# Fetches of pre_u's rows add to cleared tiles instead of copying into them, in a four-layer graph network

## The chip, the cores and the metric

The kernel runs on one core of a Trainium2 chip. The metric is device time in microseconds, measured over several executions; the median of 9 is 3608.16 us (3602.16 to 3622.97). The engines are TensorE (PE, with its weight loads as PEld), VectorE (DVE), ScalarE (ACT), GpSimd (POOL) and SyncE (SP). All values are float32.

## The reference, cut to what matters

The input x holds 64 graphs of 256 nodes with 256 features; adj is one sparse 256x256 matrix for all of them. Layers 0, 1 and 3 are of one kind, layer 2 is an attention over all nodes.

```python
def gnn(h, adj, W1, b1, W2, b2, Wa, ba, Wm, bm, beta1, beta2, beta3):
    pre_u = h @ W1[:256]
    pre_v = h @ W1[256:]
    hidden = relu(pre_u[:, :, None, :] + pre_v[:, None, :, :] + b1)   # one row per pair of nodes (u, v)
    S = sigmoid((hidden @ W2)[..., 0] + b2[0])
    a = einsum('buv,bud->bvd', S * adj, h)
    m = einsum('uv,bud->bvd', adj, h) * h
    return beta1 * h + beta2 * (a @ Wa + ba) + beta3 * (m @ Wm + bm)

x = gnn(x, layer 0); x = gnn(x, layer 1); x = attention(x); x = gnn(x, layer 3)
```

S is needed only where adj is not zero. For each edge (u, v) the kernel must form one row of 256 values, pre_u[u] + pre_v[v] + b1, take the relu, and multiply with W2.

## The kernel before

Two graphs are worked on at a time as a pair, and two pairs are under way side by side: side a takes pairs 0, 4, 8 and so on, side b pairs 2, 6, 10. `beside` joins the scores of one side ("heavy") with all other steps of the other side ("light") into one instruction order, which every engine keeps. One such round is called a block below. There are 96: 32 pairs times three GNN layers, in the order layer 0 of a, layer 0 of b, layer 1 of a, layer 1 of b, layer 3 of a, layer 3 of b. These six are called A0, B0, A1, B1, A3 and B3. Beside B1 and A3 the light steps hold an attention.

The edges of the matrix are sorted into 16 tiles of up to 128 edges, and a tile holds the edge rows of both graphs (128 partitions by 2 x 256). There are two ways to fill a tile. Eight tiles (`FAST`) are made by TensorE: ScalarE puts rows of pre_u and pre_v into the tile pre (`rows_u`, line 727, and `rows_v`, line 736), and one product with the 0/1 matrix pick gives the sums (line 675). The other eight (`FETCHED`) are gathered by GpSimd from two tables in DRAM. SyncE writes pre_u and pre_v with b1 to these tables (line 613), and `fetch` issues two indirect DMAs per tile (line 719): one copies the u rows into the tile, and one adds the v rows (`compute_op=(ALU.bypass, ALU.add)[x]`). A small ninth tile, left, holds edges that fit nowhere else and is filled in the same two steps.

`FETCHES` fixes the order of these 18 issues per block: four u fetches, four v fetches, then left's u, three u, left's v, one u and the last four v. The first eight use only the first 128 table rows. They are issued in `before`, right after these rows are written, and their tiles are called fetched of their side. The other ten are issued at the start of `scores`, and go to a fetched tile that both sides share. GpSimd works in this order and waits, where it must, for the table (SP's DMA), for the u rows of the same tile, and for the readers of a tile that is used again.

VectorE reads each edge row once (line 639: relu, times W2, summed into raw). `got` walks the eight fetched tiles, `made` the eight products. Then `rated_all` turns the sums into scores on ScalarE (lines 659 and 660), once for the first half of the tiles (EARLY) and once for the second (LATE), and VectorE multiplies them with the edges' weights into rm (line 667). In the next block, where this side is the light one, `spread` (line 763) brings rm back to matrix form with matmuls, VectorE adds it into sa (line 765), and `finish` goes on with sa (line 278), aT (line 338), the products with Wm and Wa (line 360 or 346), the new hT (line 363) and h. `before` of the next layer then computes pre_u and pre_v (line 608), evacuated as pu by ScalarE (line 609) and pv by VectorE (line 610).

Of the kernel before, what the change touches and what calls it, by code (L numbers as in the profile page):

```python
# [14 lines left out]
P = 128  # L15
# [60 lines left out]
def adj_seq_kernel(ctx: ExitStack, tc: tile.TileContext, a: dict, out: bass.AP):  # L76
# [186 lines left out]
    def stages(pools):  # L263
        fm, wk, one, ps, ga = (pools[k] for k in ("fm", "wk", "one", "ps", "ga"))


        feats = [one.tile([P, 2, D + 2], FP, name=f"f{g}") for g in range(2)]
        for f in feats:
            nc.gpsimd.memset(f[:, :, D + 1 : D + 2], 1.0)
# [59 lines left out]
        def finish(st, l):  # L329

            sa, mT = st["sa"], st["mT"]
            few_scores = l == GNN[1]
            hb = kept(st, l)
            aT = one.tile([P, 2, 2, N], FP, tag="aT", name="aT")
            for g in range(2):
                t = psum()
                product(t, st["h"][g], sa[:, :, g, :])
                nc.scalar.copy(aT[:, :, g, :], t)  # L338
                yield 0 if few_scores else 1
            if l == LAST:  # L340
                for g in range(2):
                    z = psum()
                    for m in range(2):
                        for j, (w, y) in enumerate(((wm[l], mT), (wa[l], aT))):
                            for c in range(2):
                                mm(out=z[:, m, :], lhsT=y[:, c, g, blk(m)], rhs=w[:, c, :],  # L346
                                   start=j == 0 and c == 0, stop=j == 1 and c == 1)
                        yield m * (1 + g), 1
                    o = h_tile(st, g)
                    nc.vector.tensor_tensor(o, hb[:, g], z, ALU.add)  # L350
                    nc.sync.dma_start(
                        out=out[bass.ds(st["b"] + g, 1)].rearrange("b (c p) d -> p (b c) d", p=P), in_=o
                    )
                return
            hT = hT_tile(st)
            for m in range(2):
                z = psum()
                for j, (w, y) in enumerate(((wm[l], mT), (wa[l], aT))):
                    for c in range(2):
                        mm(out=z, lhsT=w[:, c, blk(m)], rhs=y[:, c], start=j == 0 and c == 0, stop=j == 1 and c == 1)  # L360
                    if j == 0:
                        yield 0
                nc.vector.tensor_tensor(hT[:, m], hb[:, m], z, ALU.add)  # L363
                yield m if few_scores else (2 * m, 1)
            st["hT"] = hT
            st["h"] = []
            for g in range(2):
                t = psum()
                flip(t, hT[:, :, g, :])
                h = h_tile(st, g)  # L370
                if l == GNN[1]:

                    nc.vector.tensor_tensor(h, t, bias2.unsqueeze(1).to_broadcast([P, 2, D]), ALU.add)
                else:
                    nc.scalar.copy(h, t)
                st["h"].append(h)
                yield 0 if few_scores else (g, 1)
# [62 lines left out]
                    yield 0, 1  # L440
                st["h"].append(h)

        return dict(psum=psum, product=product, load=load, mixed=mixed, finish=finish, attention=attention)

    def few(stack):
        pools = open_pools(stack)
        wk, one, ga = pools["wk"], pools["one"], pools["ga"]
        s = stages(pools)  # L450
        psum, mixed, finish, attention, load = (s[k] for k in ("psum", "mixed", "finish", "attention", "load"))

# [9 lines left out]
        ids_v = one.tile([P, len(FETCHED)], I32, name="ids_v")  # L464
        left_u = one.tile([P, 1], I32, name="left_u")
        left_v = one.tile([P, 1], I32, name="left_v")
        tables = stack.enter_context(tc.tile_pool(name="tables", bufs=1, space=bass.MemoryType.DRAM))
        diag = one.tile([P, 2, N], FP, name="diag")
        nc.gpsimd.affine_select(
# [4 lines left out]
        def edges():  # L474
            scratch = Scratch(*(
                (one.tile([P, n * 2 * D], FP, tag=tag + "b", name="scratch"), n * 2 * D)
                for tag, n in (("pre", len(FAST)), ("fetched", FIRST))
            ))
            flat = lambda: psum().rearrange("p a b -> p (a b)")
            first, last, begin, number = numbers  # L480
            place = scratch.tile([P, P], FP, name="place")
# [103 lines left out]
        def before(st, l):  # L585

            hT = st["hT"]
            pu = one.tile([P, 2, 2, D], FP, tag="pu" + st["side"], name="pu")
            pv = one.tile([P, 2, 2, D], FP, tag="pv" + st["side"], name="pv")
            pre = one.tile([P, len(FAST), 2 * D], FP, tag="pre" + st["side"], name="pre")  # L590
            flat = lambda t: t.rearrange("p m g d -> p m (g d)")
            order = [(m, g) for m in range(2) for g in range(2)]
            if l == LAST:
                order = [(m, g) for g in range(2) for m in range(2)]
            st["tables"] = [
                tables.tile([N, 2 * D], FP, tag="table" + t + st["side"], name="table" + t) for t in "uv"
            ]

            own = one.tile([P, 2, 2, D], FP, tag="own", name="own")
            st["pu"], st["pv"], st["pre"], st["own"] = pu, pv, pre, own  # L600
            t = one.tile([P, FIRST, 2, D], FP, tag="fetched" + st["side"], name="fetched")
            st["fetched"] = [t[:, f] for f in range(FIRST)]
            for m, g in order:
                if l == LAST and (m, g) == (1, 0):
                    st["flip"](1)
                t = psum()
                for c in range(2):
                    mm(out=t, lhsT=hT[:, c, g, blk(m)], rhs=w1[l][:, c], start=c == 0, stop=c == 1)  # L608
                nc.scalar.copy(pu[:, m, g, :], t[:, 0, :])  # L609
                nc.vector.tensor_tensor(pv[:, m, g, :], t[:, 1, :], b1row[l], ALU.add)  # L610
                if g == 1:
                    for rows, x in zip(st["tables"], (pu, pv)):
                        nc.sync.dma_start(out=rows[blk(m)], in_=flat(x)[:, m])
                    if m == 0:
                        st["fetches"] = list(FETCHES)

                        if numbered:
                            fetch(st, 2 * FIRST)
                nc.vector.tensor_tensor(own[:, m, g, :], t[:, 0, :], pv[:, m, g, :], ALU.add)
                if g == 1:  # L620
                    if m == 0:
                        rows_u(st, 0, 2, 0, 0)
                    rows_v(st, 2 - 2 * m, 2, 0)
                yield 0, (m, g) != order[1]
            yield REST_OF_IT
            yield from mixed(st, l)

        def scores(st, l):
# [17 lines left out]

            own = st["own"]
            st["left"] = left = one.tile([P, D], FP, tag="left", name="left")
            t = one.tile([P, len(FETCHED) - FIRST, 2, D], FP, tag="fetched", name="fetched")
            st["fetched"] += [t[:, f] for f in range(len(FETCHED) - FIRST)]  # L650
            fetched = st["fetched"]
            fetch(st, len(FETCHES))

            def tile_scores(t, k, m, i):
                col = BLOCKS + 16 * m + 4 * k + i
                both(t, col, col + 8)
# [30 lines left out]
            def got(made):  # L687
                for f, block in enumerate(FETCHED):
                    if f == FIRST:
                        for _ in made:  # L690
                            yield
                        rated(left, REST)
                        rated_all(EARLY, 0)
                        yield
                    tile_scores(fetched[f], *block)
                    if f == FIRST + 1:
                        early(st)
                    yield

            def end():  # L700
                rated_all(LATE, 1)
                past.append(st["rated"].ins)

            made = made()
            return made, got(made), end

        def fetch(st, n):

            now, st["fetches"] = st["fetches"][:n], st["fetches"][n:]
            for f, x in now:  # L710
                rows = st["tables"][x]
                if f < 0:
                    to, ids = st["left"], (left_u, left_v)[x]
                    rows = rows.rearrange("n (g d) -> (n g) d", g=2)
                else:
                    to, ids = st["fetched"][f].rearrange("p g d -> p (g d)"), (ids_u, ids_v)[x][:, f : f + 1]
                    if f < FIRST:
                        rows = rows[blk(0)]
                nc.gpsimd.indirect_dma_start(  # L719
                    out=to, out_offset=None, in_=rows, in_offset=bass.IndirectOffsetOnAxis(ap=ids, axis=0),  # L720
                    compute_op=(ALU.bypass, ALU.add)[x],
                )

        def rows_u(st, f, n, k, m):
# [87 lines left out]
        for _ in steps(a_[0]):  # L812
            pass
        edges()
        numbered.append(True)
        other_weights(one, psum)
        while a_[1] is not None:
# [105 lines left out]
```

## Time and profile before

| | |
|---|---|
| median of 9 executions | 3608.16 us (3602.16 to 3622.97) |
| profiled execution | 3604.12 us, its span 3602.3 us |
| TensorE clock granted, mean | 0.989 |
| busy: PE, DVE, ACT, POOL | 3472.6, 2604.4, 1599.5, 2228.8 us |
| HBM traffic | 162 GB/s over the span |

The page of a profile gives the busy time of each engine, the DMA queues, and groups of equal instructions: line, engine, operation, output and inputs, number, busy time, mean of one in ns, and after the second bar the time in which the engine was idle just before them, with what ended it. Other views show the same trace as a timeline, or as busy times per stretch. A record on POOL is the time in which GpSimd issues one indirect DMA; the rows land later, which only the DMA's own packet records or a waiting engine show.

### The profile page before, as it was taken

To read this page: it belongs to the slowest core of one execution; us is meant where nothing else is said; L and a number is where in the kernel's file an instruction comes from. 1 tells how busy PE (TensorE), PEld (TensorE's weight loads), DVE (VectorE), ACT (ScalarE), POOL (GpSimd) and SP (SyncE) were. 2 spreads that over 40 slices of the span, in tenths; PEclk is the share of its full clock that TensorE was granted. 3 is DMA by queue.
4 is the path that set the end of the run, shared out by engine and by line. 5 is a ranking of instruction groups with operands and counts; after the bars stand their busy time and mean duration, and the time that the engine had idled before them with its cause. 6 is when DMAs were issued, how large, how long until landed. Compare 5 with 4: busy or idle time off the path is not lost. (4 is left out here: it accounts for less than half of the span.)

```text
span 3602.3 us, 48531 instructions
## 1 busy us (share of the span) xinstructions
PE 3472.6 (96%) x14328; PEld 2116.3 (59%) x14328; DVE 2604.4 (72%) x10584; ACT 1599.5 (44%) x2929; POOL 2228.8 (62%) x1754
## 2 busy tenths in 40 slices
PE   7999999999999999999999999999999999999998
PEld 4555565655656556565565656556565665655555
DVE  5667676776767777777776767768677777777676
ACT  2444444444444444444444444444444444444352
POOL 3746657576665756566576665765757566665754
PEclk8999999999999999999999999999999999999999
DMA  5757677686777767677687776867767676776865
GB/s 153 166 140 178 156 166 166 150 181 153 179 155 172 167 144 187 150 177 177 146 184 157 171 171 151 180 156 178 160 156 176 149 183 151 175 174 143 182 149 114
DMA packets 303918, 587.27 MB, mean 163 GB/s; under 512 B 37536, under 2 KB 103968, under 8 KB 303648
## 3 DMA queue, kind: packets, MB, share of 16 engines
q0 software_dynamic: 190464, 427.93, 58.8%
q1 hardware_dynamic: 111600, 154.96, 12.4%
q8 instruction: 117, 1.92, 0.2%
q14 instruction: 153, 1.25, 0.1%
q10 hardware_dynamic: 1584, 1.20, 0.1%
HBM read 466.51 MB, written 117.44 MB: 162 GB/s over the span
## 5 line engine op out<-in xcount | busy, mean ns | idle before, releaser
L719 POOL DMA_INDIRECT fetched<-tableu,ids_u x768 | 767.2, 999 | 987.5 <-DMA tableu<-pu 773.3
L719 POOL DMA_INDIRECT fetched<-tablev,ids_v x768 | 1207.3, 1572 | 257.5 <-issue 235.6
L675 PE MATMUL ga<-pre,pick 128*128 128x512 f32 x1536 | 768.1, 602 | 5.8 <-DVE junk L639 3.2
L639 DVE SCALAR_TENSOR_TENSOR junk<-ga,L_gnn_w2row 128x256 f32<-128x256 f32 x1536 | 584.9, 420 | 158.1 <-PE ga L675 127.3
L608 PE MATMUL ps<-L_gnn_w,hT 128*128 128x512 f32 x1536 | 689.3, 598 | 8.7 <-DMA hT<-in_xT_dram 8.7
L639 DVE SCALAR_TENSOR_TENSOR junk<-fetched,L_gnn_w2row 128x256 f32<-128x256 f32 x1536 | 606.9, 419 | 41.1 <-DMA fetched<-tablev,ids_v 39.7
L736 ACT COPY pre<-pv 64x512 f32<-64x512 f32 x768 | 473.4, 616 | 106.6 <-DVE pv L610 73.9
L608 PEld LDWEIGHTS ps<-L_gnn_w,hT 128*128 128x128 f32 x1536 | 288.8, 192 | 355.9 <-issue 331.4
L278 PE MATMUL ps<-sa,h 128*128 128x256 f32 x1536 | 393.6, 398 | 66.3 <-DVE sa L765 50.7
L278 PEld LDWEIGHTS ps<-sa,h 128*128 128x128 f32 x1536 | 290.7, 196 | 219.2 <-DVE sa L765 110.3
L727 ACT COPY pre<-pu 64x1024 f32<-64x1024 f32 x384 | 392.9, 1038 | 3.8
L363 DVE TENSOR_TENSOR hT<-hb,ps 128x512 f32<-128x512 f32 x128 | 88.1, 688 | 414.3 <-PE ps L360 312.1
L675 PEld LDWEIGHTS ga<-pre,pick 128*128 128x128 f32 x1536 | 277.9, 191 | 166.4 <-issue 130.5
L278 PE MATMUL ps<-adj,h 128*128 128x256 f32 x1536 | 359.0, 386 | 4.0 <-PE ps L278 1.8
L278 PEld LDWEIGHTS ps<-adj,h 128*128 128x128 f32 x1536 | 283.2, 190 | 73.7 <-issue 27.5
L609 ACT COPY pu<-ps 128x256 f32<-128x256 f32 x384 | 141.7, 372 | 413.4 <-PE ps L608 356.4
L324 ACT ACTIVATE hb<-hT,L_gnn_zbias,scas 128x512 f32<-128x512 f32 x128 | 97.4, 807 | 498.8 <-DVE hT L363 348.8
L338 ACT COPY aT<-ps 128x512 f32<-128x512 f32 x192 | 112.4, 586 | 442.5 <-PE ps L278 395.7
L667 DVE TENSOR_TENSOR rm<-gva,val 128x256 f32<-128x256 f32 x768 | 284.1, 419 | 1.7
L360 PE MATMUL ps<-aT,L_gnn_Wa 128*128 128x512 f32 x512 | 240.6, 592 | 0.0
L360 PE MATMUL ps<-mT,L_gnn_Wm 128*128 128x512 f32 x512 | 240.6, 592 | 0.0
L763 PEld LDWEIGHTS ps<-rm,gu 128*64 128x64 f32 x3072 | 175.4, 138 | 107.2 <-issue 52.4
(155 smaller groups left out, 4186.4 us busy)
## 6 DMA issues: line engine op xcount, KB each, us to landing
tableu<-pu SPq DMA_DIRECT2D x192, 256.0 KB
tablev<-pv SPq DMA_DIRECT2D x192, 256.0 KB
h<-in_x_dram SPq DMA_DIRECT2D x64, 256.0 KB
hT<-in_xT_dram SPq DMA_DIRECT2D x64, 256.0 KB
out_dram<-h SPq DMA_DIRECT2D x64, 256.0 KB
fetched<-tableu,ids_u POOLq DMA_INDIRECT x768
fetched<-tablev,ids_v POOLq DMA_INDIRECT x768
L_gnn_w<-in_L_gnn_W_dram SPq DMA_DIRECT2D x6, 256.0 KB
```

What stands on the lines that cost most here:

```text
L278: mm(out=o[:, m, :], lhsT=lhs[:, c, blk(m)], rhs=rhs[:, c, :], start=c == 0, stop=c == 1)
L338: nc.scalar.copy(aT[:, :, g, :], t)
L360: mm(out=z, lhsT=w[:, c, blk(m)], rhs=y[:, c], start=j == 0 and c == 0, stop=j == 1 and c == 1)
L608: mm(out=t, lhsT=hT[:, c, g, blk(m)], rhs=w1[l][:, c], start=c == 0, stop=c == 1)
L609: nc.scalar.copy(pu[:, m, g, :], t[:, 0, :])
L639: nc.vector.scalar_tensor_tensor(junk, t, 0.0, w2row[l], ALU.max, ALU.mult, accum_out=raw[:, i : i + 1])
L667: nc.vector.tensor_tensor(rm[:, k, ms, g, :], gva[:, k, ms, :], val[:, i : i + 4].unsqueeze(2).to_broadcast([P, 4, 64]), ALU.mult)
L675: mm(out=t, lhsT=pick[:, k, 4 * m + i, :], rhs=pre[:, n], start=True, stop=True)
L719: nc.gpsimd.indirect_dma_start(out=to, out_offset=None, in_=rows, in_offset=bass.IndirectOffsetOnAxis(ap=ids, axis=0), compute_op=(ALU.byp ...
L727: nc.scalar.copy(st["pre"][h, f : f + n], st["pu"][h, m].rearrange("p g d -> p (g d)").unsqueeze(1).to_broadcast([64, n, 2 * D]),)
L736: nc.scalar.copy(st["pre"][halves[1 - k], n], st["pv"][halves[i % 2], i // 2].rearrange("p g d -> p (g d)"))
L763: mm(out=t[h, :, quarter(i)], lhsT=gu[:, k, 4 * m + i, :], rhs=rm[:, k, 4 * m + i], start=True, stop=True)
```

## The change

The u fetches add as well, so a tile must be zero before its first fetch. The fetched tiles are three fixed tiles now, ahead for each side (tiles 0 to 3) and behind for both (tiles 4 to 7). ScalarE clears them in halves by copying a column of zeros, broadcast: ahead in `before`, placed behind the last copy of aT (`done`), and behind in `end`, placed after the late scores. The left tile is filled as before: its u rows are copied. The scratch memory of `edges` uses the side b tile of ahead in place of its predecessor.

```diff
@@ stages
+        done = []
...
-                nc.scalar.copy(aT[:, :, g, :], t)
+                done.append(nc.scalar.copy(aT[:, :, g, :], t).ins)
@@ few
+        zero = one.tile([P, 1], FP, name="zero")
+        nc.gpsimd.memset(zero, 0.0)
+        ahead = {side: one.tile([P, FIRST, 2 * D], FP, name="ahead" + side) for side in "ab"}
+        behind = one.tile([P, len(FETCHED) - FIRST, 2 * D], FP, name="behind")
+
+        def place_of(st, f):
+            return (ahead[st["side"]], f) if f < FIRST else (behind, f - FIRST)
+
+        def fetched(st, f):
+            t, f = place_of(st, f)
+            return t[:, f].rearrange("p (g d) -> p g d", g=2)
+
+        def clear(t, start, end):
+            nc.scalar.copy(t[:, start:end], zero.unsqueeze(2).to_broadcast([P, end - start, 2 * D]))
@@ before
-            t = one.tile([P, FIRST, 2, D], FP, tag="fetched" + st["side"], name="fetched")
-            st["fetched"] = [t[:, f] for f in range(FIRST)]
+            for f in range(0, FIRST, 2):
+                with tc.issue_after(done[-1]) if done else nullcontext():
+                    clear(ahead[st["side"]], f, f + 2)
@@ scores
-            t = one.tile([P, len(FETCHED) - FIRST, 2, D], FP, tag="fetched", name="fetched")
-            st["fetched"] += [t[:, f] for f in range(len(FETCHED) - FIRST)]
-            fetched = st["fetched"]
             fetch(st, len(FETCHES))
...
-                    tile_scores(fetched[f], *block)
+                    tile_scores(fetched(st, f), *block)
...
             def end():
                 rated_all(LATE, 1)
                 past.append(st["rated"].ins)
+                with tc.issue_after(past[-1]):
+                    for f in (0, 2):
+                        clear(behind, f, f + 2)
@@ fetch
-                    to, ids = st["fetched"][f].rearrange("p g d -> p (g d)"), (ids_u, ids_v)[x][:, f : f + 1]
+                    to, ids = fetched(st, f).rearrange("p g d -> p (g d)"), (ids_u, ids_v)[x][:, f : f + 1]
...
-                    compute_op=(ALU.bypass, ALU.add)[x],
+                    compute_op=ALU.bypass if (f, x) == (-1, 0) else ALU.add,
@@ after edges()
+        for f in (0, 2):
+            clear(behind, f, f + 2)
```

More of the change, by code (lines that the diff above doesn't have):

```diff
@@ L441, in attention @@
                 st["h"].append(h)
-        return dict(psum=psum, product=product, load=load, mixed=mixed, finish=finish, attention=attention)
+        return dict(psum=psum, product=product, load=load, mixed=mixed, finish=finish, attention=attention, done=done)
     def few(stack):
@@ L450, in few @@
         s = stages(pools)
-        psum, mixed, finish, attention, load = (s[k] for k in ("psum", "mixed", "finish", "attention", "load"))
+        psum, mixed, finish, attention, load, done = (
+            s[k] for k in ("psum", "mixed", "finish", "attention", "load", "done")
+        )
         pick = one.tile([P, 2, 8, P], FP, name="pick")
@@ L476, in edges @@
                 (one.tile([P, n * 2 * D], FP, tag=tag + "b", name="scratch"), n * 2 * D)
-                for tag, n in (("pre", len(FAST)), ("fetched", FIRST))
-            ))
+                for tag, n in (("pre", len(FAST)),)
+            ), (ahead["b"].rearrange("p f d -> p (f d)"), FIRST * 2 * D))
             flat = lambda: psum().rearrange("p a b -> p (a b)")
```

## The prediction

> **What bounds the kernel now.** Four views, in this order. First the page: busy shares, queues, costliest groups.
>
> ```profile
> PE 3472.6 (96%) x14328; PEld 2116.3 (59%) x14328; DVE 2604.4 (72%) x10584; ACT 1599.5 (44%) x2929; POOL 2228.8 (62%) x1754
> q0 software_dynamic: 190464, 427.93, 58.8%
> L719 POOL DMA_INDIRECT fetched<-tableu,ids_u x768 | 767.2, 999 | 987.5 <-DMA tableu<-pu 773.3
> L719 POOL DMA_INDIRECT fetched<-tablev,ids_v x768 | 1207.3, 1572 | 257.5 <-issue 235.6
> L727 ACT COPY pre<-pu 64x1024 f32<-64x1024 f32 x384 | 392.9, 1038 | 3.8
> ```
>
> TensorE (PE) is busy 96% of the span, so there are 130 us in all to win. Whatever makes PE wait is lost for good, because its order is fixed. POOL looks half free, but that is a mean over two sorts of rounds. Second, the groups by shape hold the same two operations on another tile, half as large:
>
> ```profile
> L719 POOL DMA_INDIRECT left<-tablev,left_v x96 | 151.1, 1574 | 35.8 <-issue 26.5 <-DMA fetched<-tableu,ids_u 4.6 <-DMA left<-tableu,left_u 4.4
> L719 POOL DMA_INDIRECT left<-tableu,left_u x96 | 95.8, 998 | 29.3 <-issue 15.2 <-DVE junk L639 12.8 <-DVE hb L320 0.9
> ```
>
> An issue costs POOL 1.0 us when it copies and 1.57 us when it adds, at 1 KB a row as at 2 KB. Third, one turn of six blocks, cut where POOL starts a block (A0, B0, A1, B1, A3, B3: side and layer):
>
> ```profile
> 2043.15:2075.78 32.63, 31.67 (x138) 20.67 (x137) 24.69 (x102) 14.45 (x25) 23.10 (x18) 1.00 0.82 190
> 2075.78:2108.84 33.06, 32.41 (x129) 18.47 (x129) 24.65 (x103) 15.61 (x28) 22.95 (x19) 1.00 0.77 167
> 2108.84:2141.64 32.80, 30.54 (x118) 16.93 (x116) 22.76 (x94) 14.86 (x26) 22.97 (x18) 1.00 0.75 165
> 2141.64:2185.85 44.21, 44.21 (x191) 27.10 (x189) 32.38 (x134) 21.31 (x42) 23.14 (x19) 1.00 0.60 138
> 2185.85:2228.89 43.04, 42.91 (x182) 26.20 (x181) 32.16 (x128) 19.85 (x40) 23.48 (x19) 1.00 0.66 153
> 2228.89:2260.20 31.31, 31.21 (x138) 20.74 (x136) 21.05 (x85) 11.57 (x21) 24.14 (x18) 1.00 0.81 190
> ```
>
> The columns are length, then busy time of PE, PEld, DVE, ACT, POOL, the clock, the DMA share and GB/s. POOL works 23 us in each block, plus 18 gaps of 0.30 us that it has between two issues: 28.5 us. Four of six blocks are only 31 to 33 us long. The two long ones have the attention beside them. Fourth, the timeline of block A0, from its first fetch to its last reader:
>
> ```profile
> 2043.15 0.99 POOL L719 DMA_INDIRECT fetched<-tableu,ids_u  x1 [3.83 <-DMA tableu<-pu]
> ...
> 2069.89 1.54 POOL L719 DMA_INDIRECT fetched<-tablev,ids_v  x1 [0.30 <-issue]
> 2075.78 0.99 POOL L719 DMA_INDIRECT fetched<-tableu,ids_u  x1 [4.35 <-DMA tableu<-pu]
> 2075.82 0.43 DVE L639 SCALAR_TENSOR_TENSOR junk<-fetched,L_gnn_w2row 128x256 f32<-128x256 f32 x1 [1.56 <-DMA fetched<-tablev,ids_v]
> ...
> 2079.68 1.10 DVE L667 TENSOR_TENSOR rm<-gva,val 128x256 f32<-128x256 f32 x3
> 2080.83 0.19 PEld L763 LDWEIGHTS ps<-rm,gu 128*64 128x64 f32 x2 [0.39 <-DVE rm L667]
> 2081.76 1.09 PE L763 MATMUL ps<-rm,gu 128*64 128x128 f32 x14 [0.50 <-issue]
> ```
>
> POOL ends its last fetch at 2071.43. DVE, which had nothing else left, waits 1.56 us for the rows and starts at 2075.82. Its scores become rm through ScalarE, and PE stands still before the matmuls that read rm. So in the short rounds POOL's list of fetches is already as long as the round and is part of the path; that is the view that decides.
>
> **Removed, added, moved.** PE's, DVE's and SP's orders stay as they are but for two setup swaps. POOL's order stays, with one memset of a column more.
>
> *Issue cost.* 768 copies become adds. Per fetch that is 1572 - 999 = 573 ns. Bounds: 1532 - 942 = 0.59 us between the shortest records of each, 1548 - 964 = 0.58 between medians; below, 0, if the difference belonged to the v table and not to the add. The left rows (1574 against 998) have the same difference at half the size, which fits a cost per instruction, and I take 0.573. Per block 8 x 0.573 = 4.6 us, in all 440 us of POOL (2229 to 2669 busy).
>
> *Clears.* 386 ScalarE copies of 128x1024, not in the trace; the nearest row is line 727, 64x1024 at 1038 ns (the same length per partition). 386 x 1.04 = 401 us of ACT (1600 to 2001). Above: all on the path, 401 us; below: 0. I take 0: the two clears of ahead follow the second aT copy, after which ACT idles until DVE has hT (7.9 us in the longest such wait, 349 us over 46 waits). The two of behind follow the late scores (line 659/660) and push back the pre copies by 2.08 us. In the timeline after block A0 the first ends at 2079.7, so at 2081.8 with the clears ahead of it, and the third FAST tile, which reads it first, is multiplied after 2083. The next aT copy has idle time before it of 2.1 to 3.7 us (median by kind). So that cover is nearly used up, and it is the first to fail.
>
> *Waits.* A u fetch now waits for ScalarE's clear (queued behind it on POOL: the rest of the block's fetches). The clears come 9 us or more ahead of the fetch that needs them (late scores done at 2078.8, first fetch into behind at 2090.5), so 0. The v add still waits for its u rows: it is issued 4 x 1.3 = 5.1 us later now, 7.4 us afterwards, so 0 even if an add of u rows lands 0.8 us later, as v rows do (packet records: 3.2 us after POOL's record against 2.5). Keeping the tiles takes away no wait that shows: POOL's waits for DVE's readers are 0.3 us each, which is its usual gap.
>
> *DMA.* In the packet records an add is 64 packets of 4 KB at 215 ns, a copy 128 of 2 KB at 212 ns, so the software queue's share falls from 58.8 to about 41%. The wait is latency, not bandwidth; I book 0 and keep up to 0.8 us of faster landing (last fetch of a block: median 3.5 us, least 2.7) for a rival.
>
> *The sum.* What I need for each kind of block is POOL's idle gap before the next block (beyond 0.3 us), the slack of the tightest of the four late tiles (DVE's first read less landing; zero where DVE waited), and PE's cover (start of the matmuls on the late rm, less the end of that rm). Medians over some 15 blocks each, by the instruction and packet records: A0 4.6, 0.1, 0.1; B0 4.4, 1.5, 0.8; A1 4.3, 1.3, 0.8; B1 15.6, 10.7, 0.9; A3 14.2, 8.9, 0.9; B3 2.8, 0.0, 0.05.
>
> A block starts when POOL is free and its table is written. Its table is written beside the block ahead of it, by matmuls that follow the spread of the block before that one; so it is as late as PE had become by then, and one block's delay reaches POOL two blocks on. Start a turn at B3, everything on time. B3's last rows are late by 4.6, PE by 4.6 - 0.05 = 4.5. A0 starts late by 4.6 - 2.8 = 1.8 (POOL not free); PE then is late by 1.8 + 4.6 - 0.2 = 6.2. B0 starts late by 4.5 (its table); PE: 4.5 + 4.6 - 2.3 = 6.8. A1 starts late by 6.2; PE: 6.2 + 4.6 - 2.1 = 8.7. B1 and A3 have 11.6 and 9.8 us of slack: nothing is added, POOL catches up, but PE stays late. So a turn is 8.7 us longer, and 16 turns make 139 us. The profiled execution took 3604.1 us (span 3602.3), 4 below the median 3608.2: 3604 + 139 = 3743, forecast 3740. Its own range: 0.5 us of landing either way enters twice a turn (16 us), 0.5 us more of cover three times (24 us): 3710 to 3765.
>
> The Trainium skill, page "DMA: Bandwidth & Descriptors", section "Anatomy of one DMA", calls descriptor generation small and says that many descriptors go out before its cost shows. By that rule the issue would cost nothing more and the sum would be 3604; the rows (999 against 1574 ns) disagree, and I follow them.
>
> **Rivals.**
> - *The lighter DMA pays part of it back.* For: the queue loses 18 points of share, and landings spread from 2.7 to 5.6 us. Against: the u adds land where v adds landed, and tables are written meanwhile. With 0.8 us off the last landing (twice a turn) and 0.8 off the landing of the table (twice): 139 - 16 x 3.2 = 88, 3692.
> - *The clears reach the path as well.* For: the cover above is thin. Against: the aT and pre copies still come in time by the rows. With half a pair (1.04 us) on the path in the 64 short blocks: 67 more, 3810.
> - *Not slower: the u add is as cheap as the copy*, the 573 ns belonging to the v table. Then POOL is unchanged, and a lighter queue could return DVE's waits for v rows (39.7 us) at most: 3565 to 3604, say 3590. Against: both tables have the same shape, and the left rows show the same step. It decides under some 0.04 us per fetch, since B3 and A0 have no slack.
>
> **How the numbers follow.** Forecast 0.66, lighter DMA 0.16, clears 0.08, cheap add 0.06; 0.04 for a slower kernel by another route. A range of 3655 to 3795 holds the first two and leaves out the last three, nearly 2 in 10. Faster or slower by over 0.2% is about what a measurement of this kernel can tell. Slower 0.94; cheap add is split 0.03 faster, 0.03 within 0.2%.
>
> **What would show it.** Right: POOL records of u fetches at 1.55 to 1.57 us; POOL's wait for tableu gone in the short blocks; DVE's wait for v rows up from 39.7 to hundreds of us; PE's busy time unchanged and its idle time up by the loss, before lines 763 and 278; B3 to A1 longer, B1 and A3 not. Wrong: u fetches at 1.0 us, PE idle behind pre or aT (clears), or landings under 3 us throughout (lighter DMA).

## The result, and the profile after

The changed kernel takes 3735.08 us (median of 10; 3729.8 to 3745.74) beside 3606.31 us (median of 31) for the kernel before: a ratio of 1.0355 with an interval of 1.0335 to 1.0376. It is slower by 129 us; the forecast was 3740.

The profiled execution took 3734.5 us, its span is 3732.8 us and its mean granted clock 0.977 (0.989 before). From the page, the busy times of the engines, the software queue, and the fetches:

```profile
PE 3525.8 (94%) x14328; PEld 2152.2 (58%) x14328; DVE 2602.9 (70%) x10584; ACT 1961.5 (53%) x3315; POOL 2666.3 (71%) x1755
q0 software_dynamic: 239616, 427.93, 73.0%
L740 POOL DMA_INDIRECT behind<-tablev,ids_v x384 | 604.6, 1575 | 117.0 <-issue 116.7
L740 POOL DMA_INDIRECT behind<-tableu,ids_u x384 | 594.3, 1548 | 117.0 <-issue 75.6
L740 POOL DMA_INDIRECT aheada<-tableu,ids_u x192 | 309.2, 1610 | 299.9 <-ACT pu L630 191.4
L740 POOL DMA_INDIRECT aheadb<-tableu,ids_u x192 | 311.3, 1621 | 279.7 <-ACT pu L630 148.9
```

A u fetch costs POOL 1548 to 1621 ns (999 before), and POOL is busy for 2666 us (2229 before). The second thing to see is the queue: the same 427.93 MB, but 49,152 packets more, which is 64 for each of the 768 changed fetches. The queue's share rose from 58.8 to 73.0%.

Next the waits (engine and line, what it waited for; us in total, times, longest):

```profile
DVE junk L660 <- DMA behind<-tablev,ids_v: 211.4, 118, 7.5
PE ps L784 <- DVE rm L685: 65.2, 98, 4.0
DVE junk L660 <- DMA left<-tablev,left_v: 55.9, 19, 4.8
PE ps L768 <- DVE own L640: 49.4, 18, 3.6
PE ps L280 <- DVE own L640: 16.7, 26, 1.2
DVE sa L786 <- PE ps L784: 1.1, 2, 0.9
```

The same view of the kernel before:

```profile
DVE sa L765 <- PE ga L675: 66.6, 55, 2.8
PE ps L278 <- DVE sa L765: 50.7, 64, 2.7
DVE junk L639 <- DMA fetched<-tablev,ids_v: 39.7, 39, 3.5
DVE sa L765 <- remote: 20.4, 13, 2.7
DVE sa L765 <- PE ps L763: 16.4, 38, 1.1
PE ps L763 <- DVE rm L667: 11.4, 14, 3.7
```

VectorE's wait for the last v rows grew from 40 to 211 us, and PE's wait for rm behind it from 11 to 65 us. Two waits are new: left's rows, and PE waiting at line 768 (the early scores, line 747 before) for VectorE's `own`. One wait is gone: sa's, 110 us on VectorE before (66.6 + 20.4 + 16.4 and 6.7 in a smaller group), and with it 51 us of PE's idle time. By line, all causes together, PE's idle time went from 24 to 70 us at line 784 (763 before), from 4 to 58 us at line 768 (747), and from 70 down to 48 us at line 280 (278).

One turn, cut where POOL starts a block (B0 is the second row; columns as in the prediction):

```profile
741.60:776.80 35.20, 34.34 (x136) 22.71 (x136) 25.26 (x104) 17.67 (x29) 27.84 (x18) 0.92 0.92 170
776.80:813.20 36.40, 35.23 (x135) 20.90 (x136) 25.70 (x109) 21.07 (x35) 27.64 (x18) 0.95 0.93 165
813.20:847.20 34.00, 31.68 (x123) 17.44 (x122) 22.67 (x94) 18.04 (x29) 27.31 (x18) 1.00 0.88 150
847.20:895.20 48.00, 45.52 (x182) 27.80 (x183) 33.38 (x139) 26.18 (x49) 27.86 (x18) 0.96 0.74 137
895.20:938.00 42.80, 42.80 (x182) 26.21 (x181) 32.06 (x129) 23.65 (x44) 27.66 (x18) 1.00 0.82 154
938.00:972.00 34.00, 31.16 (x136) 20.34 (x134) 21.52 (x87) 15.27 (x24) 27.79 (x19) 1.00 0.92 177
```

POOL now works 27.3 to 27.9 us in a block. With its gaps the list is 32.8 us long (28.4 before), and the short blocks of this turn are 34.0 to 36.4 us long. Means over all turns but the first, from POOL's first issues, in us:

| block | A0 | B0 | A1 | B1 | A3 | B3 | turn |
|---|---|---|---|---|---|---|---|
| before | 33.4 | 33.1 | 33.1 | 44.5 | 43.7 | 32.2 | 219.9 |
| after | 35.3 | 35.1 | 35.4 | 45.1 | 42.9 | 34.5 | 228.4 |

The turn is 8.5 us longer (8.7 forecast), and the four short blocks hold it. For PE the 130 us of span are 77 us more idle time (125.5 to 202.7) and 53 us more busy time. The instructions are the same; their records are longer. The granted clock stood at a half for 172 us in 27 stretches, against 80 us in 14 before. PE was busy for 140 us of these stretches (72 before), and a 128x512 matmul took 1061 ns inside them against 592 ns outside (medians). By these numbers the 68 us more that PE was busy at the half clock make some 30 of the 53 us; this is an estimate, and the rest is not explained. In the turn above the clock falls to 0.92 to 0.96 in three of six blocks.

One B3 block, 706 to 742 us in the timeline of the changed kernel, shows the new wait of line 768:

```profile
734.01 0.43 DVE L660 SCALAR_TENSOR_TENSOR junk<-left,L_gnn_w2row 128x256 f32<-128x256 f32 x1 [3.75 <-DMA left<-tablev,left_v]
...
735.64 0.70 PE L768 MATMUL ps<-ro,guo 64*128 64x256 f32 x2
...
738.16 0.43 DVE L660 SCALAR_TENSOR_TENSOR junk<-behind,L_gnn_w2row 128x256 f32<-128x256 f32 x1 [3.72 <-DMA behind<-tablev,ids_v]
738.51 0.42 DVE L631 TENSOR_TENSOR pv<-ps,L_gnn_b1row 128x256 f32<-128x256 f32 x1
...
739.18 0.42 DVE L640 TENSOR_TENSOR own<-ps,pv 128x256 f32<-128x256 f32 x1
...
739.75 1.63 PE L768 MATMUL ps<-ro,guo 64*128 64x256 f32 x6 [3.41 <-DVE own L640]
```

VectorE stands 3.72 us before the first behind tile. Queued behind that read are pv and own, which free a PSUM tile; PE stops in the middle of line 768 until own has run.

### The profile page after: what moved, and what is told of

Same layout as the page of the kernel before. It is cut to its first block, busy times and chain, and to the rows that moved or that the text cites. A ratio compares the mean times of both kernels' runs of the same rounds, so it can differ in the third digit from the quotient of the medians.

```text
span 3732.8 us, 49676 instructions
## 1 busy us (share of the span) xinstructions
PE 3525.8 (94%) x14328; PEld 2152.2 (58%) x14328; DVE 2602.9 (70%) x10584; ACT 1961.5 (53%) x3315; POOL 2666.3 (71%) x1755
## 3 DMA queue, kind: packets, MB, share of 16 engines
q0 software_dynamic: 239616, 427.93, 73.0%
## 5 line engine op out<-in xcount | busy, mean ns | idle before, releaser
L740 POOL DMA_INDIRECT behind<-tablev,ids_v x384 | 604.6, 1575 | 117.0 <-issue 116.7
L740 POOL DMA_INDIRECT behind<-tableu,ids_u x384 | 594.3, 1548 | 117.0 <-issue 75.6
L740 POOL DMA_INDIRECT aheada<-tableu,ids_u x192 | 309.2, 1610 | 299.9 <-ACT pu L630 191.4
L740 POOL DMA_INDIRECT aheadb<-tableu,ids_u x192 | 311.3, 1621 | 279.7 <-ACT pu L630 148.9
L660 DVE SCALAR_TENSOR_TENSOR junk<-behind,L_gnn_w2row 128x256 f32<-128x256 f32 x768 | 309.4, 420 | 217.8 <-DMA behind<-tablev,ids_v 211.4
L280 PE MATMUL ps<-adj,h 128*128 128x256 f32 x1536 | 396.0, 411 | 48.2 <-PE ps L768 16.8
L280 PE MATMUL ps<-sa,h 128*128 128x256 f32 x1536 | 365.2, 384 | 0.0
L740 POOL DMA_INDIRECT aheada<-tablev,ids_v x192 | 298.9, 1557 | 66.7 <-issue 46.2
L740 POOL DMA_INDIRECT aheadb<-tablev,ids_v x192 | 297.2, 1548 | 63.5 <-issue 48.5
L784 PE MATMUL ps<-rm,gu 128*64 128x128 f32 x3072 | 231.1, 282 | 69.5 <-DVE rm L685 65.2
```

The costliest lines, as they stand in the source:

```text
L280: mm(out=o[:, m, :], lhsT=lhs[:, c, blk(m)], rhs=rhs[:, c, :], start=c == 0, stop=c == 1)
L660: nc.vector.scalar_tensor_tensor(junk, t, 0.0, w2row[l], ALU.max, ALU.mult, accum_out=raw[:, i : i + 1])
L740: nc.gpsimd.indirect_dma_start(out=to, out_offset=None, in_=rows, in_offset=bass.IndirectOffsetOnAxis(ap=ids, axis=0), compute_op=ALU.bypa ...
L784: mm(out=t[h, :, quarter(i)], lhsT=gu[:, k, 4 * m + i, :], rhs=rm[:, k, 4 * m + i], start=True, stop=True)
```

## The experiments

The runs fell on three chips; on which chip the pair above ran is not known. The kernel before took 3622.9 us on the first (e1, e2, e3, e6), 3554.6 us on the second (e8 to e11) and 3556.4 us on the third (r1 to r4). Ratios are to the kernel before on the same chip; absolute times are compared only within one group.

### e1: clears without adds, first chip

```diff
-                    compute_op=ALU.bypass if (f, x) == (-1, 0) else ALU.add,
+                    compute_op=(ALU.bypass, ALU.add)[x],
```

> The fixed tiles and ScalarE's clears stay, but the u fetches copy again. The issue theory (the 139 us of the prediction come from 573 ns more of POOL per u fetch): 3606, within 10 us of the kernel before, ACT busy near 1960. The clears theory (ScalarE's 362 us reach the path): 3670 to 3735. The traffic theory (an add makes twice the packets, and the fuller DMA queue delays the late rows): 3606.

Measured: 3691.29 us, ratio 1.0179 (1.0153 to 1.0205). The clears, which the prediction booked at nothing, cost some 65 us on their own here. In the waits of this run:

```profile
DVE sa L786 <- PE ga L693: 111.5, 85, 2.7
PE ps L280 <- DVE sa L786: 103.9, 97, 2.8
DVE sa L786 <- remote: 51.2, 31, 3.6
```

It is the sa wait that the kernel before has too, and larger: PE stands 104 us before line 280. In the block at 1700 us, the last matmul that sa needs ends by its record at 1704.97 us, and PE's signal arrives at 1708.12 us. The ends of matmuls in these records are modelled, so a late signal and a late matmul cannot be told apart here. r3 below is the same kernel on another chip, and changes the reading.

### e2: adds without clears, first chip

```diff
-            for f in range(0, FIRST, 2):
-                with tc.issue_after(done[-1]) if done else nullcontext():
-                    clear(ahead[st["side"]], f, f + 2)
+            if l == GNN[0] and st["b"] < 4:
+                for f in range(0, FIRST, 2):
+                    ...
@@ end
-                with tc.issue_after(past[-1]):
-                    for f in (0, 2):
-                        clear(behind, f, f + 2)
```

> The u fetches add, but the tiles are cleared only once at the start, so the tiles accumulate and the output is not the reference's. Issue theory: 3735, ACT busy back near 1600. Clears theory: 3606 to 3670. Traffic theory: 3735.

Measured: 3738.5 us, ratio 1.0323 (1.0293 to 1.0353). Without the clears the loss is nearly all there, with the waits of the changed kernel (behind's v rows 218.0 us, left's 59.6 us, line 766 for own 52.3 us). The adds carry it. The changed kernel was not run on this chip, so what the clears add is left to r1 and r2.

### e3: a longer list on POOL, nothing else, first chip

```diff
+PAD = 560
...
-                nc.gpsimd.indirect_dma_start(...)
+                with tc.issue_after(pads[-1]) if pads else nullcontext():
+                    d = nc.gpsimd.indirect_dma_start(...)
+                if f >= 0 and x == 0:
+                    with tc.issue_after(d.ins):
+                        pads.append(nc.gpsimd.memset(pad, 0.0).ins)
```

> The kernel before, with a GpSimd memset of 128x560 after each u copy, held between two issues: POOL's list gets some 0.57 us longer per u fetch, with no DMA traffic, add or clear. Issue theory: 3735 (3715 to 3765). Traffic theory and clears theory: 3606.

Measured: 3668.0 us, ratio 1.0115 (1.0091 to 1.014). That is between the theories' 3735 and 3606. The memset took 586 ns but lay partly in the gap between two issues, so the list grew by 3.3 us, not 4.6. VectorE's sa wait, which the kernel before has on the profiled chip, is absent here (0.9 us). A loss of some 42 us for 3.3 us a block left open whether the list alone can give 129 us; r4 settles that.

### e6: adds with half the bytes, first chip

```diff
+                if f >= 0 and x == 0:
+                    rows = rows.rearrange("n (g d) -> (n g) d", g=2)
+                    to = fetched(st, f)[:, 0, :]
```

> The changed kernel, its u adds fetching rows of 1 KB instead of 2 KB, so half of the u rows is left out and the output is not the reference's. An issue costs POOL the same (1574 ns against 1572 in the profile of before), and the DMA time of a u add falls to about that of the old copy. Issue theory: 3735, at most 20 us less. Traffic theory: back to 3606.

Measured: 3721.31 us, ratio 1.0267 (1.0242 to 1.0292). The queue's share is back at 59.3%, and the loss is only 17 us smaller than in e2, which has no clears. The queue's added time is a small part.

### e8: the longer pad, second chip

Against e3:

```diff
-PAD = 560
+PAD = 750
```

> The kernel before, with a POOL memset of 128x750 after each u fetch. The memset of 128x560 (586 ns) had lengthened POOL's list by only 3.3 us a block, since part of it lay in the gap between two issues; this one should add about 4.5 us, as much as the adds do. Nothing else is changed. If POOL's list alone sets the loss, as the prediction's sum has it: about +125 us over the kernel before (ratio 1.035), with PE's half-clock stretches and DVE's wait for fetched v rows (211 us) of the changed kernel. If what an add costs beyond its issue (the doubled packets, the later landing) matters too: +65 to +95 us (1.018 to 1.026), the trend of the shorter pad (+42 for 3.3 us).

Measured: 3719.49 us, ratio 1.0466 (1.0448 to 1.0483), +165 us. That is more than either theory gave. The kernel before is 50 to 70 us faster on this chip, so the change needs a yardstick on one chip (r1).

### e9 and e10: one half of the clears each, with copies, second chip

```diff
@@ e9: e1 without the clears of behind
-                with tc.issue_after(past[-1]):
-                    for f in (0, 2):
-                        clear(behind, f, f + 2)
@@ e10: e1 without the clears of ahead
-            for f in range(0, FIRST, 2):
-                with tc.issue_after(done[-1]) if done else nullcontext():
-                    clear(ahead[st["side"]], f, f + 2)
```

> The changed kernel with copying fetches, and with the clears of the two ahead tiles alone (those of behind are left out). With both clears and copying fetches the time was 65 us over the kernel before. Theory: the loss comes from the behind clears, which ScalarE runs at the start of a block, ahead of its copies into pre, and the ahead clears lie in idle time: 1.000 to 1.003 of the kernel before. Rival: it is ScalarE's busy time as such, and each half of the clears costs half: 1.008 to 1.010.

> The changed kernel with copying fetches, and with the clears of behind alone (those of the ahead tiles are left out). Theory (copies into pre pushed back by 2.07 us at the start of each of 96 blocks): 1.015 to 1.018 of the kernel before, and DVE's sa waits for PE's third to sixth ga tile as with both clears (112 us). Rival (ScalarE's busy time as such): 1.008 to 1.010.

Measured: e9 3569.51 us, 1.0044 (1.0027 to 1.0061); e10 3553.28 us, 1.0000 (0.9991 to 1.001). The theory fell, and in the wrong direction, and the rival with it: the clears of behind, at the start of a block, cost nothing on this chip, and those of ahead cost 15 us. Neither run shows the sa wait. e10 also says that fixed tiles as such cost nothing there.

### e11: left's rows one place sooner, second chip

```diff
-FETCHES += [(-1, 0), (4, 0), (5, 0), (6, 0), (-1, 1), (7, 0), (4, 1), (5, 1), (6, 1), (7, 1)]
+FETCHES += [(-1, 0), (4, 0), (5, 0), (-1, 1), (6, 0), (7, 0), (4, 1), (5, 1), (6, 1), (7, 1)]
```

> The changed kernel with left's v rows fetched one place sooner, ahead of the u rows of the third behind tile: its landing comes about 1.9 us sooner, and the list is as long as before. Theory (left's late landing is a stall of its own, 43 us of PE's idle time in the B3 blocks alone): 1.020 to 1.028 of the kernel before, and PE's idle time ahead of the early scores in B3 falls below 15 us. Rival (the last behind tiles set the end of these blocks anyway, as the prediction's sum has it): within 0.3% of the changed kernel, 1.033 to 1.038, with PE's idle time moved from the early scores to the late ones.

Measured: 3752.78 us, ratio 1.0562 (1.0545 to 1.058). The edit did not take hold. In POOL's records left's v fetch stays in thirteenth place, behind three u fetches into behind, in all blocks but one of 96. Only one u fetch follows it where the edited list has two:

```profile
734.97 1.53 POOL L740 DMA_INDIRECT behind<-tableu,ids_u  x1 [0.30 <-issue]
736.81 1.74 POOL L740 DMA_INDIRECT left<-tablev,left_v  x1 [0.30 <-issue]
738.85 1.53 POOL L740 DMA_INDIRECT behind<-tableu,ids_u  x1 [0.30 <-issue]
740.68 1.53 POOL L740 DMA_INDIRECT behind<-tablev,ids_v  x1 [0.30 <-issue]
```

So whether left's late landing is a stall of its own stays open, and the agreement with the rival's number is no evidence for it. What ran is in effect the changed kernel on the second chip, with its waits:

```profile
DVE junk L660 <- DMA behind<-tablev,ids_v: 224.0, 117, 6.2
DVE junk L660 <- DMA left<-tablev,left_v: 62.1, 23, 4.4
PE ps L768 <- DVE own L640: 56.1, 24, 3.8
```

Read so, the change costs 198 us on this chip, and the pad of e8 gives 165 us of them.

### r1 to r4: four kernels on the third chip

r1 is the changed kernel, r2 is e2, r3 is e1 and r4 is e8, all unchanged, run side by side.

> The changed kernel, untouched, as the yardstick for the three kernels run beside it on one chip: the earlier experiments ran on two chips on which the kernel before itself took 3623 and 3555 us. Theory (the list of POOL sets a floor for the short blocks, and what else slows the kernel before, which differs by chip, hides under it): about the same absolute time as elsewhere, 3730 to 3755 us, so a ratio of 1.03 on a chip where the kernel before takes 3620 and of 1.05 where it takes 3555. Rival (each microsecond of issue adds to what the chip takes anyway): a ratio of 1.035 on every chip.

> The changed kernel with its clears made only once, ahead of the first blocks (the u adds then land on the rows of an earlier block, so that part of the sum is wrong in value; instructions and traffic are those of the changed kernel but for the clears). Theory (clears lie under POOL's list): within 0.3% of the changed kernel beside it. Rival (clears cost what they cost alone, 16 to 65 us): 0.4 to 1.8% less than the changed kernel.

> The changed kernel with copying fetches and all its clears. On one chip it cost 65 us (1.018), while the ahead clears alone cost 16 us and those of behind nothing on another. Theory (the cost of the clears depends on the chip, through signals of PE that reach DVE late there): 1.00 to 1.006 if the kernel before takes some 3555 us on this chip, 1.015 to 1.02 if it takes some 3620. Rival (the two halves cost more together than apart): 1.015 to 1.02 on any chip.

> The kernel before with the 128x750 memset on POOL after each u fetch, so that POOL's list is as long as with the adds (14.8 and 17.8 us for its two parts, against 14.8 and 17.7), with copies' traffic and no clears. Theory (the longer list gives most of it): 25 to 40 us less than the changed kernel beside it, the rest being the doubled packets (the half rows gave back 17 us). Rival (the packets give half or more): over 65 us less.

| | us | ratio | interval | PE idle, us | clock at a half, us |
|---|---|---|---|---|---|
| kernel before | 3556.40 | | | | |
| r3, clears alone | 3573.77 | 1.0052 | 1.0035 to 1.007 | 105 | 63 |
| r4, pad alone | 3715.61 | 1.0446 | 1.0429 to 1.0464 | 198 | 139 |
| r2, adds alone | 3744.22 | 1.0529 | 1.0511 to 1.0547 | 211 | 169 |
| r1, the change | 3766.02 | 1.0593 | 1.0574 to 1.0611 | 220 | 185 |

The change costs 209.6 us on this chip, and three steps make it up.

*The longer list* (r4, a memset in place of the add's extra time) gives 159.2 us: 76% of the loss, with copies, their packets and no clear. The memsets did not slow VectorE: its reads of 128x256 took 418 ns with them and without.

*The adds in its place* (r2 less r4) give 28.6 us. The lists are nearly equally long (14.8 and 17.7 us for the two parts against 14.8 and 18.0 with the pad, medians), so this is about what an add does beyond its issue: the last u fetch of a block lands 3.25 us after POOL's record instead of 2.09 (medians, from the packet records). It is a net figure. With the pad A0 and A1 are 1.2 and 2.0 us longer than with the adds, and B0, B1 and B3 1.5 to 2.1 us shorter, which is not explained.

*The clears* (r1 less r2) give 21.8 us, about the 17.4 us that they cost alone. What lets them cost 22 us is not settled: PE has 10 us more idle time and 12 us more busy time, spread over several places.

By the expectations, r2's rival was right and r3's theory too. r1's 1.059 is nearer its theory's 1.05 than its rival's 1.035, and its time lies 11 us over the theory's range. r4 is 50 us below the change, between its theory (25 to 40) and its rival (over 65): the list gives most, but the rest is larger than said.

Where the adds' 29 us sit is seen in the waits, first of r4 (the early scores are line 753 there), then of r1:

```profile
DVE junk L641 <- DMA fetched<-tablev,ids_v: 233.2, 177, 4.5
PE ps L769 <- DVE rm L669: 80.2, 110, 5.0
PE ps L753 <- DVE own L621: 25.1, 15, 2.2
DVE junk L641 <- DMA left<-tablev,left_v: 21.1, 16, 2.0
```

```profile
DVE junk L660 <- DMA behind<-tablev,ids_v: 219.1, 120, 7.9
PE ps L784 <- DVE rm L685: 66.0, 100, 4.0
DVE junk L660 <- DMA left<-tablev,left_v: 59.8, 27, 4.8
PE ps L768 <- DVE own L640: 57.3, 26, 4.0
```

The pad alone makes VectorE wait as long for the last v rows as the change does. What the adds put on top is at left and at line 768, in the middle of POOL's list: in the B3 blocks left's v rows land 25.5 us after the block's start with the pad, 27.1 us in r1. The last v rows of a block land no later after POOL's record (4.25 us in r1, 4.21 with the pad, 4.09 in r3).

r3 is e1's kernel: 3691 us there, 3574 us here, with waits on sa of 185 us there (111.5 + 51.2 + 17.1 + 5.3). Of VectorE's waits on sa here only this is left:

```profile
DVE sa L786 <- PE ps L784: 0.9, 1, 0.9
```

So e1's 65 us were mostly not the clears' own. They go with a wait that two profiles of a short list show (e1 on the first chip, and the kernel before) and three do not (e9, e10 and r3, on the other two chips). No kernel with a longer list shows it on any chip.

## Why the prediction was right, and where not

**What bounds the kernel: right.** In the short blocks POOL's list left little of the block over, and time put into it came out as time: in r4 4.7 us a block, 451 us in 96 blocks, cost 159 us with nothing else changed. The list does not fill the short blocks even now. POOL still stands idle for 1.3 to 3.2 us at the end of each (3.1 to 4.9 before, medians), where the prediction's sign was that its wait for the table would be gone.

**Issue cost: right.** Forecast 1572 ns per u add and 2669 us of POOL; measured 1548 to 1621 ns and 2666 us. left's unchanged u copies still take 987 ns. The rival of a cheap u add is out. With the pad, 4.7 us more a block on POOL cost 4.5% of the time. The Trainium skill, page "DMA: Bandwidth & Descriptors", section "Anatomy of one DMA", calls descriptor generation small, by which the time would not have moved; these runs disagree.

**DMA: wrong.** The step read the packet records the wrong way round. Before, a copy was 64 packets of 4 KB and an add 128 of 2 KB. The share went up to 73.0%, not down to 41%, and the u rows land later (last u fetch of a block 3.02 us after POOL's record, 2.08 before). The rival "the lighter DMA pays back", with 0.16, had no ground. What an add does beyond its issue cost some 29 us on the third chip where the step booked 0; e6 gave back 17 us by halving the bytes. The number of packets alone could not tell the two readings apart, since a tile has 192 packets either way; the order in time of the 4 KB packets against POOL's records could have.

**Clears: size missed, place wrong.** Booked 0 in bounds of 0 to 401 us; they cost 22 us in the change on the third chip. The prediction feared those of behind, which push back the copies into pre. Beside copying fetches on the second chip, e10 shows that these cost nothing, and e9 that those of ahead, called hidden in ScalarE's idle time, cost 15 us. How the 22 us divide is not measured.

**Waits: right.** POOL's waits for u rows ahead of their v adds are 10.4 and 11.0 us for the two ahead tiles, 0.3 us for behind and 3.1 us for left, in all of 96 blocks. No wait of POOL longer than 0.3 us is put down to a clear, and a clear ends at least 15.9 us (ahead) and 6.9 us (behind, where the prediction had 9) before the first u fetch into its tile.

**The sum: right in the number, with errors of opposite sign, so in part by luck.** The recurrence gave 8.7 us a turn and the turn grew by 8.5 us. But it priced the list alone, at 139 us, and on the third chip the list alone cost 159 us, what adds do beyond their issue 29 us and the clears 22 us. There 3556 + 139 = 3695 would have stood against 3766, 71 us off. On the other side, the sum took the kernel before as it was profiled, with 110 us of VectorE's waits on sa and 51 us of PE's on them, and did not see that they would go: after shows 1.1 us of them. That a longer list goes with this, on one chip, is seen on the first: 185 us of these waits in e1, 0.9 us in e6, which has the same clears and adds its u rows (halved). On the third chip r3 has 0.9 us, so there is nothing to lose (the kernel before has no profile there). That the vanished waits make up the difference between the chips is a comparison, not an experiment; the kernel before is 50 us faster on the third chip (3556 against 3606) and the changed one 31 us slower (3766 against 3735), and those 31 us are not explained.

**Where PE would stand: one of three.** Line 763 (now 784) came as said, from 24 to 70 us. At line 278 (now 280) PE stands less than before, 48 us for 70, and no longer for sa: 17 us of it are waits for own. Line 768 in the B3 blocks (49 us for own) was missed. The step followed the late rows to rm and on to PE, but not to what stands behind the waiting read in VectorE's queue, pv and own, whose PSUM PE needs. On the third chip the missed place holds over half: from r3 to r1 PE's idle time grew by 115 us, 63 of them at line 768, 43 at line 280 and 6 at line 784, where r3 already waits 60 us.

**PE's busy time unchanged: wrong.** It rose by 53 us, some 30 of them by the clock at a half.

## What to carry to other kernels

When a queue of issues is nearly as long as the stage it serves, price a change by what it adds to that queue, and test the price with a dummy instruction of the same length: the 745 ns memset gave three quarters of the loss. Check in the trace that an edit moved what it was to move: e11's did not, and its time alone would have passed for an answer. Follow a late transfer not only to its reader but to all that is queued behind the reader, since there it holds PSUM that PE waits for. And count what the kernel before loses to other waits, since a new bound can hide them. This one change measured 3.5% on one chip and 5.9% on another; that hidden waits are all of the difference is not shown.

## What was not expected of the hardware

- An accumulating gather of 128 rows of 2 KB went out as 128 packets (209 ns each on average), a copying one as 64 packets of 4 KB (215 ns): near twice the queue's time for the same bytes. Halving the bytes of the added rows brought the share from 74.4 to 59.3% but left POOL's time for the issue as it was.
- PE was granted half the clock more often: 14 stretches (80 us) before, 27 (172 us) after, 23 (139 us) with the pad alone. They follow its stalls: 25 of the 27 begin within 6 us after PE stood for over 1 us (13 of the 14 before), and only 9% of all instants lie so (6% before). On the profiled pair 77 us more of idle time went with an estimated 30 us more of slow matmuls.
- VectorE waited for signals of PE that came 3.15 us after the recorded, modelled end of the matmul (e1), in two profiles of kernels whose POOL list is short. One kernel on two chips waited 185 us for them and 0.9 us. The cause was not found.
